# A two-layer graph attention kernel: the order of work in its first two and last two batches

## The chip, the core and the metric

The kernel runs on one NeuronCore of a Trainium2 chip. The core has five engines with queues of their own: TensorE (PE in the profile; its weight loads are PEld), VectorE (DVE), ScalarE (ACT), GpSimd (POOL) and SyncE (SP), which here only issues DMAs. Each engine works through its own list of instructions in order and waits at semaphores for the others. The metric is the device time of one execution in microseconds (us), the median of several runs.

## What is computed

32 graphs of 512 nodes, 512 features, one adjacency matrix for all. All data are float32.

```python
# layer 0: graph attention, 512 -> 256 features, joined with h
h = X @ W
e = leaky_relu(h @ a[0] + (h @ a[1]).T, 0.2) + NEG * (1 - adj)
x = layernorm(X + concat([softmax(e) @ h, h]))
# layer 1: 8 heads of 64, masked
q, k, v = (x @ Wq.T + bq), (x @ Wk.T + bk), (x @ Wv.T + bv)     # split into heads
scores = where(adj == 0, -inf, q @ k.T / 8)
x = layernorm(x + (softmax(scores) @ v) @ Wo.T + bo)
```

## The kernel before

One graph is a batch `b`. Its 512 nodes lie as 4 tiles of 128 rows, its features as 4 chunks of 128. The body at the end of the function is a program written out by hand: an opening (L892 to L925), a loop over 32 batches and the four head pairs `hp` of each (L941 to L1050), and an end (L1051 to L1056). All five engines keep the order in which these calls issue instructions (`manual_schedule`, L101), so the text order is the queue order on each engine.

**Layer 0.** `l0_project` multiplies a tile of x-transposed (`xt`) with `w_sb` into PSUM (`ph`, L276 by `matmul_f`) and ScalarE copies it to `h`. `w_sb` carries two more columns, `W @ a`, computed first (`pa`, L183). `l0_maxima`, `l0_scores` and `l0_weights` make the masked exponents `et`; `l0_values` multiplies them with `h` (`po`, L480) and adds to x; `l0_add_h` adds h to the other half of x on GpSimd; `ln_stats`, `ln_root` and `l0_norm` are the layer norm. For batch 0 rows are turned by TensorE (`row_of`: `pn`, `pself`, `pl`), for later ones through DRAM.

**Layer 1.** x is turned: for batch 0 by TensorE (`x1_first`: `px` L512, copied by ScalarE at L513), for later ones by VectorE in 32x32 blocks (`x1_blocks`) and 16 DMAs (`move_one`, L348). The products with the weights use a Strassen-like scheme with seven instead of eight block products: `x1_sums` makes four sums of x blocks (`tx`), `weight_sums` the sums of the weights (`wqx_sb`, `wkx_sb`, `wvx_sb`; `output_sums` for `wox_sb`), one quarter of each weight is negated by ScalarE. `project_two` gives q and k of two pairs (`pw`, L548), `project_v` v (`pv`, L624), `finish_seven` the output product (`pf`, L772) as a generator of ten steps that the loop calls one by one.

**A head pair.** `head_scores` computes 128 rows for two heads (`ps`, L701), VectorE subtracts the maximum under the mask (`minus_max`, L324) and ScalarE takes the exponent with its sum (L710). `head_blocks` turns the eight 128x512 blocks: VectorE in 32x32 blocks (L339), then 16 DMAs of 128 KB (`move_pair`, L356) put the blocks in place in `pt`. They go by SP; for pair 2 of batch 0 and the last two pairs of the last batch also by GpSimd and ScalarE. The sums are inverted, written to DRAM (L721) and read back to all partitions (`head_inverse`, L731, issued by GpSimd). One pair later `head_values` multiplies `pt` with v (`pav`, L740), and VectorE scales the result (L752).

**The end.** The output of the last batch isn't done by seven products: `finish` multiplies three chunks under the last pair's DMAs and the fourth after it (L841), then VectorE adds x, takes the statistics and normalises, tile by tile.

**Buffers.** `ps_m` and `ps_s` are four PSUM banks each, handed round by the tags "m" and "s". `t` and `pt` have one buffer each, so a pair's VectorE blocks wait until the pair before has been moved, and a move waits for the `pav` before.

```python
            if hp == 2 and b == 0 or hp >= 2 and not more:
                queues.append(nc.gpsimd)
            if not more and hp == 3:
                queues.append(nc.scalar)
            head_blocks(b, hp, queues)
            if before is not None:
                head_values(*before)
```

Of the kernel before, what the change touches and what calls it, by code (L numbers as in the profile page):

```python
# [14 lines left out]
P = 128  # L15
G = 32
# [10 lines left out]
def kernel(  # L27
# [123 lines left out]
    nc.sync.dma_start(w_sb[:, :, 2:], w.rearrange("(c p) o -> p c o", p=P))  # L151
# [3 lines left out]
    a_sb = const.tile([P, OC, 2], F32, name="a_sb")  # L155
    nc.sync.dma_start(a_sb, a)
    load_xt(0)
    adj_sb = prob.tile([P, NB, N], adj.dtype, name="adj_sb", tag="t", bufs=1)
    nc.sync.dma_start(adj_sb, adj.rearrange("(c p) n -> p c n", p=P))
    load_x(0)  # L160
    for dst, src in ((wq_sb, wqt), (wk_sb, wkt), (wv_sb, wvt)):
        nc.sync.dma_start(dst, src.rearrange("(c p) d -> p c d", p=P))
    load_xt(1)

    adjp_sb = act.tile([P, NB, N], adj.dtype, name="adjp_sb", tag="x1t")
# [59 lines left out]
    def weight_sums():  # L225

        for c in range(FC):
            nc.scalar.activation(wq_sb[:, c, :], wq_sb[:, c, :], AF.Identity, scale=SCALE)  # L230
        pairs = "p c (s i d) -> p i c s d"
        for w_t, x_t, view, s in (
            (wq_sb, wqx_sb, pairs, 2),
            (wk_sb, wkx_sb, pairs, 2),
            (wv_sb, wvx_sb, "p c (s i d) -> p i c (s d)", 1),
        ):
            v = w_t.rearrange(view, s=s, i=2)
            lo, hi = slice(0, FC // 2), slice(FC // 2, FC)

            i, j = (1, 0) if s == 2 else (0, 1)  # L240
            a11, a21 = v[:, i, lo], v[:, j, lo]
            a12, a22 = v[:, i, hi], v[:, j, hi]
            s1, s2, s4 = (x_t[:, i] for i in range(3))
            nc.vector.tensor_tensor(s1, a21, a22, ALU.add)
            nc.scalar.activation(a22, a22, AF.Identity, scale=-1.0)
            nc.vector.tensor_tensor(s2, s1, a11, ALU.subtract)
            yield
            nc.vector.tensor_tensor(s4, a12, s2, ALU.subtract)
            nc.vector.tensor_tensor(a21, a11, a21, ALU.subtract)
            yield  # L250

    def output_quarters():
        v = wo_sb.rearrange("p c (i d) -> p i c d", i=2)
        lo, hi = slice(0, FC // 2), slice(FC // 2, FC)
        return v[:, 0, lo], v[:, 0, hi], v[:, 1, lo], v[:, 1, hi]

    def output_sums():

        a11, a12, a21, a22 = output_quarters()
        s1, s2, s4 = (wox_sb[:, i] for i in range(3))  # L260
        nc.gpsimd.tensor_tensor(s1, a21, a22, ALU.add)
        nc.gpsimd.tensor_tensor(s2, s1, a11, ALU.subtract)
        nc.gpsimd.tensor_tensor(s4, a12, s2, ALU.subtract)
        nc.gpsimd.tensor_tensor(a21, a11, a21, ALU.subtract)
        nc.scalar.activation(a22, a22, AF.Identity, scale=-1.0)

    def output_weights():

        a11, _, a21, a22 = output_quarters()
        nc.gpsimd.tensor_tensor(a21, a11, a21, ALU.subtract)  # L270
        nc.scalar.activation(a22, a22, AF.Identity, scale=-1.0)
# [6 lines left out]
    def psum(name):  # L278
        return ps_m.tile([P, N], F32, name=name, tag="m")

# [71 lines left out]
    def move_pair(dst, t, queues):  # L352

        for g in range(4):
            for r in range(4):
                queues[(4 * g + r) % len(queues)].dma_start(  # L356
                    dst[r * G : (r + 1) * G, g], t[g * G : (g + 1) * G, r]
                )
# [8 lines left out]
    def l0_project(b, i):  # L367

        if i == 0:
            h_sb = act.tile([P, NB, F1 + 3], F32, name=f"h_{b}", tag="h")  # L370
            nc.gpsimd.memset(h_sb[:, :, F1 + 2 :], 1.0)
            st["h", b] = h_sb
        xt_sb, h_sb = st["xt", b], st["h", b]
        ph = ps_m.tile([P, 2 + F1], F32, name=f"ph_{b}_{i}", tag="m")
        matmul_f(ph, lambda c: xt_sb[:, c, i * P : (i + 1) * P], lambda c: w_sb[:, c, :])
        nc.scalar.copy(h_sb[:, i, : F1 + 2], ph)
# [20 lines left out]
    def l0_maxima(b):  # L397
# [4 lines left out]
        if b == 0:  # L402
            pn, mask = psum("pn"), st["mask0"]
# [41 lines left out]
    def l0_scores(b, tiles=range(NB)):  # L445

        h_sb = st["h", b]
        if b == 0:
            pself = psum("pself")
# [14 lines left out]
    def l0_row_first():  # L464
        most, row = st["least", 0], psum("pl")
# [9 lines left out]
    def l0_values(b, i):  # L475
        h_sb, z = st["h", b], st["x1", b]
        et = st["et", b]
        po = ps_m.tile([P, F1 + 1], F32, name=f"po_{b}_{i}", tag="m")
# [25 lines left out]
    def x1_first():  # L504
# [3 lines left out]
        for i in range(NB):  # L508
            px = psum(f"px_{i}")
# [177 lines left out]
    def head_scores(b, hp, i):  # L687
        qk = st["qk", b, hp]
        if i == 0:
            st["t", b, hp] = prob.tile(  # L690
                [P, 4, 2, FC, NB, G], F32, name=f"t_{b}_{hp}", tag="t", bufs=1
            )
# [3 lines left out]
        t, total = st["t", b, hp], st["tot", b, hp]  # L696
        pss = []
        for j in range(2):
            rows = slice(j * D, (j + 1) * D)
            ps = ps_s.tile([P, N], F32, name=f"ps_{b}_{hp}_{i}_{j}", tag="s")  # L700
# [14 lines left out]
    def head_blocks(b, hp, queues=(nc.sync,)):  # L715
        t, total = st.pop(("t", b, hp)), st.pop(("tot", b, hp))
        for j, i, p in st.pop(("p", b, hp)):
            transpose_blocks(t[:, :, j], i, p)
# [3 lines left out]
        st["inv", b, hp] = d  # L722
        pt = prob.tile([P, 4, 2, FC, NB, G], F32, name=f"pt_{b}_{hp}", tag="pt", bufs=1)
        move_pair(pt, t, queues)
# [111 lines left out]
    def finish(b, i, chunks=range(FC)):  # L836
        if 0 in chunks:
            st["pf", b, i] = psum(f"pf_{b}_{i}")
        ps, z = st["pf", b, i], st["x1", b]
        for c in chunks:  # L840
            nc.tensor.matmul(  # L841
                ps,
                st["ot", b, c // 2][:, c % 2, i * P : (i + 1) * P],
                wo_sb[:, c, :],
                start=(c == 0),
                stop=(c == FC - 1),
            )
        if FC - 1 not in chunks:
            return
        nc.vector.tensor_tensor(z[:, i, :], ps, z[:, i, :], ALU.add)  # L850
        o = out[b].rearrange("(c p) f -> p c f", p=P)
        layernorm(z, f"1_{b}_{i}", [i])
# [44 lines left out]
    l0_add_h(0)  # L897
    l0_row_first()
    l0_weights(0)
    nc.vector.tensor_scalar(bqs_sb, bq_sb, SCALE, None, ALU.mult)  # L900
    sums = weight_sums()
    next(sums)
    next(sums)
    for i in range(NB):
        l0_values(0, i)
        ln_stats(st["x1", 0], "0_0", i)
        ln_root("0_0", [i])
        if i > 0:
            l0_norm(0, [i - 1])
    l0_norm(0, [NB - 1])  # L910
    next(sums)
    next(sums)
    masks1()
    l0_project(1, 0)
    l0_project(1, 1)
    x1_first()
    l0_project(1, 2)
    l0_project(1, 3)
    l0_columns(1)
    x1_sums(0, nc.vector)  # L920
    steps(sums)
    steps(project_two(0, 0))
    l0_maxima(1)
    l0_write(1)
    l0_read(1)  # L925
    def l0_output(b):
# [13 lines left out]
    before = None  # L940
    for b in range(B):  # L941
        more = b < B - 1
        seven = finish_seven(b - 1) if b > 0 else None
        for hp in range(NP):
# [5 lines left out]
            if hp == 0:  # L950
                values = project_v(b)
                next(values)
                if more:
                    l0_scores(b + 1, [0, 1])
            elif hp == 1:
# [11 lines left out]
            else:  # L967
                if b > 0:
                    if not more:
                        steps(seven)  # L970
                        output_weights()
                    out_stats(b - 1)
                else:
                    output_sums()
# [13 lines left out]

            queues = [nc.sync]
            if hp == 2 and b == 0 or hp >= 2 and not more:  # L990
                queues.append(nc.gpsimd)
            if not more and hp == 3:
# [123 lines left out]
```

## Time and profile before

| what | value |
|---|---|
| three runs, us | 3106.84, 3104.37, 3106.60; median 3106.6 |
| profiled execution, us | 3105.46, of which its span is 3103.7 |
| mean granted TensorE clock | 0.991 |
| busy share: PE, PEld, DVE, ACT, POOL | 98%, 66%, 81%, 49%, 40% |
| chain that ended last | PE 91%, DVE 2%, DMA 2% |
| busy in 0 to 30 us: PE, DVE, ACT, POOL | 16.86, 12.76, 8.35, 9.17 |
| busy in 30 to 55 us | 19.86, 14.85, 9.18, 0.10 |
| busy in 3042 to 3082 us | 29.84, 23.38, 16.39, 14.65 |
| busy in 3082 to 3103.7 us | 8.94, 9.88, 1.18, 0.00 |

In the profile a group of instructions is written as line, engine, operation, output tile <- input tiles, shape and count; times run from the start of the span. In brackets stands how long the engine had been idle before, and who released it. A float32 matmul appears as two records, a transpose by TensorE as one.

### The profile page before, as it was taken

The numbers are of one execution on the slowest core, as the hardware profiler recorded it, in microseconds if no ns is written. First come the engines' busy times: TensorE is split into PE (matmuls) and PEld (weight loads), VectorE is DVE, ScalarE is ACT, GpSimd is POOL, SyncE is SP. The second block draws the span as 40 slices with busy tenths as digits, with TensorE's granted clock in tenths as the row PEclk, the third lists the DMA queues.
The fourth block names the chain that finished last, engine by engine and source line by source line (L and its number), as shares of the span: only waits on it lengthen the run. The fifth ranks groups of instructions, "written<-read, shape, count | busy, mean of one in ns | idle before, by whom it ended". The sixth has DMA issues, their size and how long they took to land.

```text
span 3103.7 us, 44628 instructions
## 1 busy us (share of the span) xinstructions
PE 3033.9 (98%) x13356; PEld 2058.0 (66%) x13356; DVE 2516.3 (81%) x5735; ACT 1527.4 (49%) x3246; POOL 1250.3 (40%) x1237
## 2 busy tenths in 40 slices
PE   7899999999999999999999999999999999999996
PEld 6566676666666666666666666666666666666653
DVE  5788788887788888788888888888888888888865
ACT  3445544455544455555455445455444555444542
POOL 1444444434444433434443434343444344444322
PEclk9999999999999999999999999999999999999998
DMA  5556665666665666755665756666656666656544
GB/s 163 123 141 161 154 163 140 160 154 156 163 155 136 167 154 151 172 143 142 162 162 142 176 140 154 153 163 150 165 138 160 153 158 162 153 139 166 141 120 113
DMA packets 247936, 470.92 MB, mean 152 GB/s; under 512 B 95568, under 2 KB 98128, under 8 KB 247696
## 3 DMA queue, kind: packets, MB, share of 16 engines
q1 hardware_dynamic: 233984, 430.82, 56.7%
q0 software_dynamic: 13472, 36.59, 4.5%
q8 instruction: 108, 1.77, 0.3%
q14 instruction: 132, 1.08, 0.1%
q10 hardware_dynamic: 240, 0.66, 0.1%
HBM read 132.65 MB, written 34.27 MB: 54 GB/s over the span
## 4 chain that ended last, share of the span: by engine, by line
PE 91%; DVE 2%; DMA 2%; SPq 1%; POOL 1%; issue 1%; ACT 0%; DVEq 0%; POOLq 0%; ACTq 0%
PE pw L548 24%; PE pav L740 14%; PE ps L701 14%; PE pf L772 12%; PE pv L624 12%; PE po L480 7%; PE ph L276 7%; SPq L356 1%; DMA pt<-t 1%; DVE t L339 1%; DMA d_least<-least 1%; DVE p L324 1%; DVE qk L585 0%; POOL x L795 0%; DVE stats L289 0%
## 5 line engine op out<-in xcount | busy, mean ns | idle before, releaser
L710 ACT ACTIVATE p<-p,least 128x512 f32<-128x512 f32 x1024 | 725.8, 711 | 517.1 <-DVE least L324 210.0
L324 DVE CUSTOM_DVE_ANT_0 p<-ps,mask 128x512 f32<-128x512 f32 x1024 | 644.7, 685 | 212.4 <-PE ps L701 212.3
L339 DVE STREAM_TRANSPOSE t<-p 128x512 f32<-128x512 f32 x1024 | 622.8, 674 | 14.2 <-issue 7.2
L701 PE MATMUL ps<-qk 64*128 64x512 f32 x2048 | 514.6, 617 | 3.8 <-DVE qk L585 3.4
L740 PE MATMUL pav<-pt,v 128*64 128x512 f32 x2048 | 474.8, 606 | 29.0 <-DMA pt<-t 16.9
L740 PEld LDWEIGHTS pav<-pt,v 128*64 128x64 f32 x2048 | 140.9, 138 | 348.6 <-issue 306.2
L731 POOL DMA_DIRECT2D inv<-d_tot x256 | 133.1, 525 | 559.1 <-DMA d_tot<-tot 297.9
L701 PEld LDWEIGHTS ps<-qk 64*128 64x128 f32 x2048 | 180.4, 186 | 211.9 <-issue 150.5
L462 POOL TENSOR_TENSOR et<-et,mask0t 128x512 f32<-128x512 f32 x126 | 143.8, 1153 | 327.1 <-ACT et L458 327.1
L480 PE MATMUL po<-h,et 128*128 128x257 f32 x1024 | 237.3, 390 | 6.7 <-ACT et L473 4.4
L276 PE MATMUL ph<-w_sb,xt 128*128 128x258 f32 x1024 | 235.8, 388 | 2.3 <-ACT x1t L513 2.0
L480 PEld LDWEIGHTS po<-h,et 128*128 128x128 f32 x1024 | 193.1, 194 | 63.4 <-issue 25.9
L795 POOL TENSOR_TENSOR x<-x,u_o 128x512 f32<-128x512 f32 x93 | 117.0, 1272 | 285.3 <-ACT u_o L790 254.9
L276 PEld LDWEIGHTS ph<-w_sb,xt 128*128 128x128 f32 x1024 | 194.1, 192 | 54.0 <-PE ps L701 22.0
L295 ACT ACTIVATE rstd<-mv,eps 128x4 f32<-128x4 f32 (+1 forms) x70 | 20.7, 297 | 357.3 <-DVE mv L290 352.8
L537 POOL TENSOR_TENSOR x<-x,bo_sb 128x512 f32<-128x512 f32 x128 | 158.4, 1269 | 91.2 <-DVE x1t_b L339 91.1
L710 ACT ACTIVATION_READ_ACCUMULATOR p<-p,least 128x1 f32 x1024 | 192.3, 188 | 0.0
L710 ACT ACT_TABLE_LOAD x63 | 80.8, 1283 | 221.5 <-DVE least L324 221.0
L772 PE MATMUL pf<-wo_sb,ot 128*128 128x256 f32 x744 | 182.9, 389 | 0.0
L289 DVE BATCH_NORM_STATS2 stats<-x 128x6 f32<-128x512 f32 x256 | 174.6, 682 | 6.1 <-POOL x L795 1.2
L772 PEld LDWEIGHTS pf<-wo_sb,ot 128*128 128x128 f32 x744 | 136.7, 190 | 63.9 <-issue 24.2
L772 PE MATMUL pf<-wox_sb,ot 128*128 128x256 f32 x744 | 179.1, 383 | 0.0
(145 smaller groups left out, 5346.8 us busy)
## 6 DMA issues: line engine op xcount, KB each, us to landing
pt<-t SPq DMA_DIRECT2D x2022, 128.0 KB, 3.5
x<-in_x_dram SPq DMA_DIRECT2D x32, 1024.0 KB, 5.7
inv<-d_tot POOLq DMA_DIRECT2D x256, 128.0 KB, 3.9
xt<-in_xt_dram SPq DMA_DIRECT2D x31, 1024.0 KB, 5.6
x1t<-x1t_b SPq DMA_DIRECT2D x496, 64.0 KB, 2.0
out_dram<-x SPq DMA_DIRECT2D x31, 1024.0 KB, 5.8
rows<-d_att SPq DMA_DIRECT2D x31, 512.0 KB, 4.0
rows<-d_least SPq DMA_DIRECT2D x31, 256.0 KB, 4.7
```

The source lines that it names most:

```text
L276: nc.tensor.matmul(ps, lhs(c), rhs(c), start=(c == 0), stop=(c == FC - 1))
L289: nc.vector.bn_stats(stats, z[:, i, :])
L324: nc.vector.tensor_tensor_reduce(out=out, in0=scores, in1=mask, scale=-1.0, scalar=MIN_INIT, op0=ALU.add, op1=ALU.min, accum_out=least,)
L339: nc.vector.transpose(t[:, :, :, i, :].rearrange("p r c q -> p c r q"), src.rearrange("p (c r k) -> p c r k", r=4, k=G),)
L480: nc.tensor.matmul(po, et[:, j, i * P : (i + 1) * P], h_sb[:, j, 2:], start=(j == 0), stop=(j == NB - 1),)
L537: nc.gpsimd.tensor_tensor(z[:, i, :], z[:, i, :], bo_sb, ALU.add)
L548: nc.tensor.matmul(ps[:, k * half : (k + 1) * half], weights(k, c), moving(c), start=start and k == 0 and c == 0, stop=c == FC // 2 - 1, s ...
L624: nc.tensor.matmul(ps[:, k * half : (k + 1) * half], columns(k, c), weights(c), start=start and k == 0 and c == 0, stop=c == FC // 2 - 1, ...
L701: nc.tensor.matmul(ps, qk[rows, 0, i * P : (i + 1) * P], qk[rows, 1, :], start=True, stop=True)
L710: nc.scalar.activation(p, p, AF.Exp, bias=least, scale=-1.0, accum_out=total[:, j, i : i + 1])
L740: nc.tensor.matmul(po[j * D : (j + 1) * D, :], st["v", b, c // 2][:, c % 2, head * D : (head + 1) * D], pt[:, :, j, c, :, :].rearrange("p ...
L772: nc.tensor.matmul(ps[:, k * half : (k + 1) * half], columns[:, c, k * P : (k + 1) * P], weights(c), start=start and k == 0 and c == 0, st ...
```

## The change

1. Loads: `a`, `wt`, `w` instead of `w`, `wt`, `a`; xt of batch 1 straight behind `adj`, before x of batch 0; the key weights before the query weights. The second form of the mask (`adjp_sb`) shares a buffer with `adj_sb` under the tag "t", no longer with x1t.
2. `l0_project` is split into product and copy. Two of batch 1's four products stand after `l0_add_h(0)`, one after `l0_row_first`, one after the last `l0_values` of batch 0; the ScalarE copies follow together. Batch 0's other PSUM tiles of layer 0 move to `ps_s`.
3. Sums of the key and query weights run on GpSimd, those of the value weights on VectorE after `x1_sums`; ScalarE's negations are calls of their own. `masks1` and `l0_maxima(1)` stand later; `l0_add_h(1)` earlier.
4. The output weight's negation moves from before batch 0's last projection to the end of pair 3. Pair 2 of batch 0 is moved by SP alone.
5. Pairs (30, 2), (31, 2) and (31, 3) are turned by TensorE (`head_turn`), into `ps_s` banks, and copied out by VectorE and ScalarE in turns. No blocks and no DMAs for them.
6. For batches 30 and 31 the last steps of `finish_seven` run in pair 3; in batch 31 its GpSimd step stands after `project_two` instead of before it.
7. The last output: x is added in PSUM by a product with the identity, statistics are read from PSUM, and ScalarE normalises from PSUM, one tile behind.

```diff
-    nc.sync.dma_start(w_sb[:, :, 2:], w.rearrange("(c p) o -> p c o", p=P))
+    a_sb = const.tile([P, OC, 2], F32, name="a_sb")
+    nc.sync.dma_start(a_sb, a)
...
+    nc.sync.dma_start(w_sb[:, :, 2:], w.rearrange("(c p) o -> p c o", p=P))
     load_xt(0)
...
     nc.sync.dma_start(adj_sb, adj.rearrange("(c p) n -> p c n", p=P))
+    load_xt(1)
     load_x(0)
-    for dst, src in ((wq_sb, wqt), (wk_sb, wkt), (wv_sb, wvt)):
+    for dst, src in ((wk_sb, wkt), (wq_sb, wqt), (wv_sb, wvt)):
...
-    load_xt(1)
...
+    def weight_sums(which, engine):
+
+        a11, a12, a21, a22 = weight_quarters(which)
+        s1, s2, s4 = (which[1][:, i] for i in range(3))
+        engine.tensor_tensor(s1, a21, a22, ALU.add)
+        engine.tensor_tensor(s2, s1, a11, ALU.subtract)
+        engine.tensor_tensor(s4, a12, s2, ALU.subtract)
+        engine.tensor_tensor(a21, a11, a21, ALU.subtract)
+
+    def weight_negative(which):
+
+        a22 = weight_quarters(which)[3]
+        nc.scalar.activation(a22, a22, AF.Identity, scale=-1.0)
...
+    def head_turn(b, hp):
+
+        pt = prob.tile([P, 4, 2, FC, NB, G], F32, name=f"pt_{b}_{hp}", tag="pt", bufs=1)
+        for k, (j, i, p) in enumerate(st.pop(("p", b, hp))):
+            ps = psum_s(f"pt_{b}_{hp}_{i}_{j}")
+            for c in range(FC):
+                cols = slice(c * P, (c + 1) * P)
+                nc.tensor.transpose(ps[:, cols], p[:, cols], ident)
+            (nc.vector.tensor_copy if k % 2 == 0 else nc.scalar.copy)(
+                pt[:, :, j, :, i, :].rearrange("p g c q -> p c g q"),
+                ps.rearrange("p (c g q) -> p c g q", c=FC, g=4),
+            )
+        head_sums(b, hp)
+        st["pt", b, hp] = pt
...
+    def last_products(b, i):
+
+        ps = st["pf", i] = psum(f"pf_{b}_{i}")
+        nc.tensor.matmul(ps, ident, st["x1", b][:, i, :], start=True, stop=False)
+        for c in range(FC - 1):
+            last_product(b, i, c)
...
+    def last_norm(b, i):
...
+        nc.vector.bn_stats(stats, ps)
+        nc.vector.bn_aggr(mv, stats)
+        nc.scalar.activation(rstd, mv[:, 1:2], AF.Sqrt, bias=eps)
+        yield
+        nc.vector.reciprocal(rstd, rstd)
+        nc.vector.scalar_tensor_tensor(shift, mv[:, 0:1], -1.0, rstd, ALU.mult, ALU.mult)
+        nc.scalar.activation(z[:, i, :], ps, AF.Identity, bias=shift, scale=rstd)
         nc.sync.dma_start(o[:, i, :], z[:, i, :])
...
     l0_add_h(0)
+    second = [l0_product(1, 0), l0_product(1, 1)]
     l0_row_first()
+    second.append(l0_product(1, 2))
     l0_weights(0)
...
-    sums = weight_sums()
-    next(sums)
-    next(sums)
+    for c in range(FC):
+        nc.scalar.activation(wq_sb[:, c, :], wq_sb[:, c, :], AF.Identity, scale=SCALE)
+    weight_sums(KEYS, nc.gpsimd)
+    weight_negative(KEYS)
+    weight_sums(QUERIES, nc.gpsimd)
     for i in range(NB):
         l0_values(0, i)
         ln_stats(st["x1", 0], "0_0", i)
+        if i == NB - 1:
+            second.append(l0_product(1, 3))
+            for k in range(NB):
+                l0_copy(1, k, second[k])
...
-    masks1()
-    l0_project(1, 0)
-    l0_project(1, 1)
     x1_first()
-    l0_project(1, 2)
-    l0_project(1, 3)
     l0_columns(1)
     x1_sums(0, nc.vector)
-    steps(sums)
-    steps(project_two(0, 0))
+    weight_sums(VALUES, nc.vector)
+    masks1()
+    two = project_two(0, 0)
+    next(two)
+    weight_negative(VALUES)
+    next(two)
+    next(two)
     l0_maxima(1)
     l0_write(1)
     l0_read(1)
+    steps(two)
...
+    turned = {(B - 2, 2), (B - 1, 2), (B - 1, 3)}
...
+                if b == 0:
+                    l0_add_h(1)
...
+                    if b + 2 >= B:
+                        steps(seven)
                     if not more:
-                        steps(seven)
                         output_weights()
...
-                    output_sums()
+                    weight_sums(OUTPUT, nc.gpsimd)
...
-            queues = [nc.sync]
-            if hp == 2 and b == 0 or hp >= 2 and not more:
-                queues.append(nc.gpsimd)
-            if not more and hp == 3:
-                queues.append(nc.scalar)
-            head_blocks(b, hp, queues)
+            if (b, hp) not in turned:
+                head_blocks(b, hp)
             if before is not None:
                 head_values(*before)
+            if (b, hp) in turned:
+                head_turn(b, hp)
...
-                if b > 0:
+                if b > 0 and more:
                     next(seven)
...
+                if not more:
+                    next(seven)
...
                 if b == 0:
+                    weight_negative(OUTPUT)
                     add_bias(1)
...
     for i in range(NB):
-        finish(b, i, range(FC - 1))
-    head_values(b, 3, lambda name: ps_s.tile([P, N], F32, name=name, tag="s"))
+        last_products(b, i)
+    head_values(b, 3, psum_s)
+    norms = []
     for i in range(NB):
-        finish(b, i, [FC - 1])
+        last_product(b, i, FC - 1)
+        norms.append(last_norm(b, i))
+        next(norms[i])
+        if i > 0:
+            steps(norms[i - 1])
+    steps(norms[NB - 1])
```

## The prediction

> **What bounds the kernel.** I read the two strips of the page first, TensorE's busy share and its granted clock, in 40 slices.
>
> ```profile
> span 3103.7 us, 44628 instructions
> PE   7899999999999999999999999999999999999996
> PEclk9999999999999999999999999999999999999998
> ```
>
> TensorE is full from the second slice to the last but one. The table of stretches shows 100.00 busy in each 100 us that I asked for between 190 and 2945 (one: 99.46). The change leaves the order of that middle alone, so I expect nothing there, and only the first 155 us and the last 160 us count. The timeline of TensorE gives its waits there (start, length, instruction, idle before and releaser):
>
> ```profile
> 49.21 6.30 PE L276 MATMUL ph<-w_sb,xt 128*128 128x258 f32 x16 [2.04 <-ACT x1t L513]
> 55.35 1.02 PE L548 MATMUL pw<-x1t,wq_sb 128*128 128x256 f32 x4
> ...
> 93.41 8.98 PE L480 MATMUL po<-h,et 128*128 128x257 f32 x28 [3.27 <-ACT et L473]
> ...
> 149.72 5.46 PE L740 MATMUL pav<-pt,v 128*64 128x512 f32 x16 [6.19 <-ACT h L376]
> ```
>
> ```profile
> 2968.93 5.56 PE L740 MATMUL pav<-pt,v 128*64 128x512 f32 x16 [6.79 <-DMA pt<-t]
> 3033.40 2.99 PE L701 MATMUL ps<-qk 64*128 64x512 f32 x8 [3.37 <-DVE qk L585]
> 3061.41 5.40 PE L740 MATMUL pav<-pt,v 128*64 128x512 f32 x16 [5.82 <-DMA pt<-t]
> 3081.89 5.35 PE L740 MATMUL pav<-pt,v 128*64 128x512 f32 x16 [3.16 <-DMA pt<-t]
> ```
>
> The first block is the opening: half of batch 1's projection runs late (6.30 us for 16 records, where 32 take 7.24 later), the first `pw` follows it, then come two long waits. The second is the end: three waits for blocks that DMA turns, one for a sum on GpSimd. Each wait costs more than itself: 16 records of L740 take 3.65 us elsewhere and 5.4 here. The stretches of 0.5 us (length, TensorE busy, clock, DMA) say why:
>
> ```profile
> 23.50:24.00 0.50, 0.00 (x0) 1.00 1.04 385
> 27.00:27.50 0.50, 0.00 (x0) 0.60 1.07 262
> 33.50:34.00 0.50, 0.50 (x3) 0.57 1.12 221
> ```
>
> The clock falls to 0.50 at 27.1, after idle 22.0 to 25.9 and 26.5 to 28.7, and is back at 33.9, so 5.2 us of matmuls run at half pace. The falls near 47.6, 92.0, 2966, 3058 and 3082 look alike and hold it down for 3.4 to 5.2 busy us: a gap of 3 us or more costs another **1.7 to 2.6 us**.
>
> **Opening, up to the first `pw`.** Up to 22.0 the start hangs on adj landing at 16.6; the reordered loads keep adj behind the same 2 MB. Then:
> - Two tiles of the second projection stand before `pl` (25.89): 16 of 32 records that take 7.24 us warm, 3.6 us, fill 22.0 to 25.6. The third (1.8 us) fills 26.5 to 28.3. The clock should stay up, so `po` runs at 1.8 us a tile from 28.7, waits for its exponents until 30.5, and ends at 36.3 instead of 38.3; the fourth ends at 38.1. xt(1) takes the place of x(0), which was issued at 7.81 and landed 11.5 later, at 19.3; x(0) moves to the next slot (10.91 + 11.1 = 22.0), before GpSimd wants it (25.1). Cost nothing while these slots hold; 3 us if xt(1) came after 25.
> - VectorE loses the query sums (32.56 to 35.23) and the key sums (44.41 to 47.07), 2.7 us each. Its norm chain starts with `po` at 31.2: 4 tiles x 1.61 us (recip, 256-wide add, stats, aggregate) + 4 x 0.66 us norms + 0.4 us for the root's table = 40.7, instead of 44.4.
> - GpSimd takes 8 sums behind its four `x+h` adds (end 28.66). Nearest row: L261 to L264, 1.27 us each, so 10.1 us to 38.8. Queued behind them is only a memset. The first wanted is the query sum, at the third product, 1.75 us after `pw` starts (41.8 below): 4.7 us slack.
> - ScalarE copies the four projections after the last exponents, with no wait for VectorE; the transposes `px` follow at 38.1 in other banks. The last x1t copy (0.51 us) ends near 41.8.
>
> [...] The row:
>
> ```profile
> 112.43 1.92 DVE L305 TENSOR_SCALAR x<-x,mv,rstd 128x512 f32<-128x512 f32 x4
> 2933.42 3.78 DVE L305 TENSOR_SCALAR x<-x,mv,rstd 128x512 f32<-128x512 f32 x4
> ```
>
> Alone, four norms take 1.92; with GpSimd working, 3.78: 0.46 us more each. Two or three norms fall beside the sums. [...] by the row 1.2 at most; I take 0.7. So `pw` starts at 42.5: **12.9 us gained.**
>
> **Opening, from `pw` to the third pair.** The 12.2 us of `pw` are unchanged. Behind it VectorE has the value sums and masks1 (3.9 us) under those products. The wait at 71.6 shrinks with 1.6 us (`ps` to the value products 6.98 us before, 5.4 now), and gaps of 0.5 go: 15.0 gained at `ps` of pair 1 (85.63, now 70.6). `x+h` of batch 1 now stands before the row on GpSimd (3.6 us), so VectorE's v results wait for the row (2.15) and the p7 sum (1.4), then come two L472, two masks (2.25) and the exponents. `po` can start near 75.5 with TensorE idle from 72.5: 3.0 us, and the clock likely falls. Before it was 4.4 us with the same fall, so +1.7 with rounding: `po` ends at 85.6 instead of 102.3, **16.7 gained**.
>
> Pair (0,2) now goes by SP alone. SP's chain from pair 1's turned blocks has no slack: 16 pt x 0.64, xt 0.6, 16 x1t 12.2, then:
>
> ```profile
> 136.71 6.01 SPq L356 DMA_DIRECT2D pt<-t  x8
> 131.93 3.91 POOL L356 DMA_DIRECT2D pt<-t  x8 [16.09 <-DMA x1t<-x1t_b]
> ```
>
> Before, GpSimd issued half, and the output sums behind these issues held ScalarE's h copies, so `pav` started at 149.72. Now 16 x 0.64 from 136.7 end at 147, landing 3.8 later (row: 2964.79, 3.84), 150.7. Moving the negation frees ScalarE, but the transfer takes that wait's place: -1.0 (bounds -3.5 and +1.5, if x1t goes faster without GpSimd's half). **Opening: 15.7.** What follows runs cold in both.
>
> **End, batch 30.** Turning pair (30,2) costs 32 transposes. 16 of L206 took 2.09 us, four of L363 start 0.44 apart; 0.11 each, 3.5 us, with one bank wait 3.7. The copies (ScalarE L513 0.51, VectorE L210 0.69, four each) lie beside. `pav` no longer waits 6.79. But the products moved to hp 3 put GpSimd's last two adds behind the inv issues and the tx sums (L527 to L530, 5.1 us from 2960): they end at 2967.6. VectorE's stats, minus-max, ScalarE's exponents and out_norm (2.9) queue behind, so the copy p1 that `pw`'s fourth product waits for comes at 2977.7; TensorE, 5.9 us ahead, idles from 2973.8 and goes cold. The last turned pair by DMA, (30,3), leaves VectorE at 2977 instead of 2973.6 and lands at 2991.9, just when `pav` wants it. **Net 0** (-1 to +3).
>
> **End, batch 31.**
> - GpSimd's `to`/`ot` sums move behind p7: it is added by 3026.4 instead of 3031.7, q and k are ready by 3028.2, `ps` follows at 3030.0: 3.37 idle and 1.8 of slow clock gone, +5.2.
> - `pav` (31,1) then waits for its DMA (issues end 3032.9, +3.8): -0.7. Turning (31,2): -3.7. `pav` (31,2) starts at once, without 5.82 idle and 1.8 slow: +7.6. Here 8.3 us ahead, `pav` ending at 3058.4.
> - Turning (31,3): ScalarE's four copies stand behind its four out_norm instructions, which end at 3064.7; transposes 6 to 8 wait for these banks, end 3066.6. TensorE goes cold (2.5).
> - The products that used to lie under the DMA wait (12 of 0.86 us) now stand alone, and 4 identity products of that shape are added: 16 x 0.86 = 13.8. Then `pav` 3.6, ot 1.1: 3087.6 against 3088.3 before. Ahead 0.7.
> - The tail. Before, ot's end to the last norm was four VectorE rounds of 2.7 us. Now VectorE has stats, aggregate, two small ones (1.2 us a tile) and ScalarE normalises from PSUM (L870 0.73, L513 0.51): 7.2 us instead of 12.0; the store's 3.4 stay. +4.8.
>
> **End: 5.5.** [...]
>
> **Sum.** 15.7 + 5.5 = 21.2. The profiled execution took 3105.46 (span 3103.7), which gives 3084.3; the median, 3106.6, is 1.1 above it: **3085.4**.
>
> **Rivals.**
> 1. Forecast, 0.60, own range 3080 to 3091.
> 2. The opening shift is eaten by SP's single queue and by `po`'s exponents: landings at 0.76 us each (the x1t pace) cost 2 more, GpSimd's row 2 to 3 more. For it: SP has no slack there. Against: less runs beside it. Gain 10.5 + 5.5: 3090.5. 0.18.
> 3. The turned pairs give their waits back: [...] 15.7 - 2: 3092.9. 0.11.
> 4. Neither gap lets the clock fall, and x1t is faster: 3079. 0.08.
> 5. Slower: [...] `pw`'s third product waits for them; beyond 4.7 us slack each us costs one. To eat 21 us they must take 4.5 us each; at 5.5 the time is 3113. Every such sum in the trace takes 1.26 to 1.5. 0.03.
>
> A difference under 0.2% (6.2 us) can't be told from no change. Faster 0.94, same 0.03, slower 0.03. The range, 3077 to 3095, leaves some 2 in 10 out.
>
> **What would show it.** First `pw` near 42 to 43 with clock 1.00 from 20 to 72; a wait at `po` of 3 us; `pav` (0,2) released by DMA pt; no idle before `pav` (30,2), but one inside `pw` of batch 31 released by ScalarE's copy; `ps` (31,2) without idle; the last store within 11 us of the last ot. I am wrong if `pw` starts after 46, or if the middle changes its pace.

## The result, and the profile after

The changed kernel takes **3078.89 us** (median of 6 runs, 3075.24 to 3080.89) against 3106.22 before (6 runs), ratio 0.9913, 95% interval [0.9901, 0.9926]: 27.3 us less, where 21.2 were forecast. That lies inside the stated range of 3077 to 3095, but 1.1 us under the forecast's own 3080 to 3091; rival 4 had named 3079. The profiled execution took 3080.21 us, with a span 25.3 us shorter than before. The strips of its page:

```profile
span 3078.4 us, 44731 instructions
...
PE   8999999999999999999999999999999999999998
...
PEclk9999999999999999999999999999999999999999
```

The last slice went from 6 to 8 and the last clock digit from 8 to 9. TensorE's timeline in the opening (start, length, instruction, idle before and releaser):

```profile
35.94 1.91 PE L264 MATMUL ph<-w_sb,xt 128*128 128x258 f32 x8
...
40.28 1.28 PE L509 MATMUL px<-ident,x 128*128 128x128 f32 x8 [1.56 <-DVE rstd L291]
42.23 2.07 PE L545 MATMUL pw<-x1t,wq_sb 128*128 128x256 f32 x4 [0.67 <-ACT x1t L510]
...
78.21 9.21 PE L477 MATMUL po<-h,et 128*128 128x257 f32 x32 [2.86 <-ACT et L470]
...
133.55 5.77 PE L757 MATMUL pav<-pt,v 128*64 128x512 f32 x16 [4.99 <-DMA d_att<-att]
```

The projection's tiles have left the place in front of `pw`, which starts 13.1 us earlier. But four records of L545 take 2.07 us there and 1.03 later: the clock is down, which it was not before. The end:

```profile
2962.88 2.05 PE L545 MATMUL pw<-tx,wqx_sb 128*128 128x256 f32 x4 [4.75 <-ACT p L569]
...
3024.83 3.90 PE L736 MATMUL pt<-ident,p 128*128 128x128 f32 x32
3028.57 1.89 PE L789 MATMUL pf<-wox_sb,ot 128*128 128x256 f32 x8
...
3046.39 1.23 PE L736 MATMUL pt<-ident,p 128*128 128x128 f32 x8 [1.23 <-DVE pt L737]
...
3063.69 3.65 PE L757 MATMUL pav<-pt,v 128*64 128x512 f32 x16
3068.49 3.70 PE L861 MATMUL pf<-wo_sb,ot 128*128 128x512 f32 x8 [1.15 <-DVE ot L769]
```

Of the four waits shown before none is left. New are 4.75 us inside batch 31's first projection, and 2.4 us in three pieces inside the turn of the last pair (the largest is shown). A turned pair costs 3.90 us, and the rows behind it run at full clock.

Where the time went, in us gained, read from the starts of the same instruction in both traces (the first four rows count from the start, the others are stretches):

| stretch | forecast | measured |
|---|---|---|
| to the first `pw` | 12.9 | 13.1 |
| to the first scores of pair (0,1) | 15.0 | 12.3 |
| to the end of `po` of batch 1 | 16.7 | 15.0 |
| to the values of pair (0,2) | 15.7 | 16.2 |
| from there to the values of (30,1) | 0 | -0.3 |
| from there to batch 31's first scores | 0 | -1.4 |
| from there to the last eight products | +0.7 | +5.4 |
| from these to the end of the span | +4.8 | +5.4 |
| sum of the last five rows | 21.2 | 25.3 |

### The profile page after: what moved, and what is told of

The parts are those of the page before. It is cut to its first block, busy times and chain, and to the rows that moved or that the text cites. A ratio compares the mean times of both kernels' runs of the same rounds, so it can differ in the third digit from the quotient of the medians.

```text
span 3078.4 us, 44731 instructions
## 1 busy us (share of the span) xinstructions
PE 3039.4 (99%) x13460; PEld 2065.7 (67%) x13460; DVE 2490.8 (81%) x5711; ACT 1537.7 (50%) x3262; POOL 1251.6 (41%) x1224
## 5 line engine op out<-in xcount | busy, mean ns | idle before, releaser
L330 DVE STREAM_TRANSPOSE t<-p 128x512 f32<-128x512 f32 x1000 | 607.7, 674 | 10.2 <-issue 5.5
```

The lines of the kernel that those rows point to most:

```text
L330: nc.vector.transpose(t[:, :, :, i, :].rearrange("p r c q -> p c r q"), src.rearrange("p (c r k) -> p c r k", r=4, k=G),)
```

## The experiments

Two limits on reading them. Runs of one kernel mostly differ by some 3 us either way, in run 12 by up to 7. And the stretch from the values of pair (0,3) to those of (30,1), the same order in all, took from 2771.7 to 2777.9 us in twelve profiled runs of kernels with the changed opening or a variant of it; why it varies isn't known. So a part of a few us is read from its own stretch of the trace, and the medians say whether the whole agrees.

**1. The opening alone.** The end is set back to the old one.

```diff
-    turned = {(B - 2, 2), (B - 1, 2), (B - 1, 3)}
+    turned = set()
...
-        last_products(b, i)
+        finish(b, i, range(FC - 1))
...
```

> The changed kernel's opening (loads, projection in the gaps, weight sums on GpSimd, masks, first move of pair 2 on one queue) with the old end: no pair is turned by TensorE, the last norm is the old one. The two ends of the kernel are 2900 us apart and share only the engines' queues. Theory 'two separate gains': the opening is worth what the two traces differ by at the first product of pair (0,2), 149.7 - 133.5 = 16.2 us, so 3106.2 - 16 = 3090 us (3088 to 3092). Rival 'one gain through the clock or the DMA queues': a part of what looks like the opening's gain only lasts to the end because the end was changed too, so under 12 us here (over 3094). A second rival, that the opening's lead is eaten in the 29 batches between: under 3 us (over 3103).

Measured 3087.52 us, ratio 0.9941 [0.9928, 0.9953], 17.9 below the runs beside it and 0.5 under the range. The gain lasts to the end by itself. TensorE's timeline in this run shows something else, though the opening is the same code:

```profile
39.41 1.28 PE L509 MATMUL px<-ident,x 128*128 128x128 f32 x8 [1.55 <-DVE rstd L291]
41.37 1.13 PE L545 MATMUL pw<-x1t,wq_sb 128*128 128x256 f32 x4 [0.68 <-ACT x1t L510]
...
75.63 7.56 PE L477 MATMUL po<-h,et 128*128 128x257 f32 x32 [2.85 <-ACT et L470]
```

The gaps are those of the changed kernel to 0.01 us, yet `pw` takes 1.13 in place of 2.07 and `po` 7.56 in place of 9.21. Here the scores of pair (0,1) come at 70.80, where 70.6 was forecast. That they agree is partly luck: `pw` is 1.1 us earlier than forecast in this run, and from it to these scores it takes 29.4 us, where 28.1 were forecast (31.1 in the changed kernel).

**2. The end alone.** The old opening, with the turned pairs and the new last norm.

```diff
+    turned = {(B - 2, 2), (B - 1, 2), (B - 1, 3)}
...
-            if hp == 2 and b == 0 or hp >= 2 and not more:
+            if hp == 2 and b == 0:
...
```

> The old opening with the changed end: pairs (30,2), (31,2) and (31,3) turned by TensorE, the last norm from PSUM. Theory 'two separate gains': what the traces differ by behind pair (30,1), -1.3 in batch 30, +5.4 from there to the last product, +5.4 in the tail, is 9.5 us, so 3106.2 - 9.5 = 3096.7 us (3095 to 3099); together with the kernel that has the opening alone the gains add up to the whole 27.3 us within 1.5 us. Rival: the end's gain hangs on the opening's rearranged buffers or queues, then the two gains add up to less than 24 us.

3095.19 us, ratio 0.9967 [0.9956, 0.9979]: 10.2 less. 17.9 + 10.2 = 28.1 against 27.3 for the whole. The two gains add up, as expected.

**3. Batch 29's norm late.**

```diff
-                    out_stats(b - 1)
+                    if b + 2 != B:
+                        out_stats(b - 1)
...
+                if b + 2 == B:
+                    out_stats(b - 1)
                 if more:
                     steps(project_two(b + 1, 0))
                 head_inverse(b, 3)
+                if b + 2 == B:
+                    ln_root(f"1_{b - 1}")
+                    out_norm(b - 1)
+                    store(b - 1)
```

> In batch 30 alone, the statistics of batch 29's last norm are put behind the values of pair (30,2) on VectorE, and its root, its four norms on ScalarE and its store behind the projection of batch 31. Theory 'queue of ScalarE': the 4.75 us idle before the fourth product of that projection (released by ScalarE's copy, which stands behind late exponentials and four norms of 2.9 us) and the cold rows behind it (2.05 + 1.91 + 1.56 us in place of 3 x 1.03) go, 4.75 + 2.4 = 7.2 us; about 1 may come back where VectorE's statistics (3.3 us) now stand ahead of the projection's results: 3071.5 to 3074, around 3072.5. Rival 'the cold clock is set elsewhere' (by the turned pair before it): the wait goes and the rows stay cold, 3074 to 3075. Rival 'the projection waits for GpSimd's sums tx anyway': under 2 us gained, over 3077.

3069.92 us, ratio 0.9888 [0.9872, 0.9903]. The timeline of the stretch (TensorE and ScalarE):

```profile
2953.59 1.03 PE L545 MATMUL pw<-tx,wk_sb 128*128 128x256 f32 x4
2954.45 1.03 PE L545 MATMUL pw<-tx,wqx_sb 128*128 128x256 f32 x4
...
2956.98 1.28 ACT L286 ACT_TABLE_LOAD   x1
...
2961.45 1.99 PE L699 MATMUL ps<-qk 64*128 64x512 f32 x8
```

No idle time ahead of the fourth product (the second row), no cold row; the root's table load comes behind the copies. From the values of (30,2) to the scores of batch 31 it takes 15.9 us (2945.59 to 2961.45) in place of 23.1 (2949.09 to 2972.23): **7.3 gained, 7.2 expected**. The profiled run gained another 3.7 us in the opening: it is the second in which the clock stayed up there (scores of pair (0,1), third and fourth tile, at 83.62; changed kernel 87.35). That would explain why the time lies under the expected range.

**4. The same stall from GpSimd's side.** The norms stay; the sums `tx` go behind the last two adds.

```diff
                     if b + 2 >= B:
                         steps(seven)
+                    if b + 2 == B:
+                        x1_sums(b + 1, nc.gpsimd)
...
-                if more:
+                if b + 2 < B:
                     x1_sums(b + 1, nc.gpsimd)
```

> The changed kernel with one order swapped on GpSimd in batch 30: the four sums tx for batch 31's projection stand behind the last two adds of batch 29's output, in place of ahead of them. The norms of batch 29 stay where they are on ScalarE. If GpSimd's order sets the stall of batch 30's end, VectorE's statistics no longer wait 3.0 us for the second add, so the exponentials, the norms and the copies come about 3 us earlier: the idle time before the projection's fourth product falls from 4.75 to about 1.7 us, and the clock behind it may stay whole: 2.5 to 5.5 us gained from the first product of that projection to the first scores of batch 31 (19.55 us in the changed kernel). If the norms in front of the copies are enough by themselves, the stretch stays at 18 us or more. If the projection now waits for tx, its third product shows a wait for GpSimd and nothing is gained.

3075.58 us, ratio 0.9898 [0.9882, 0.9915]. TensorE's timeline:

```profile
2961.01 1.10 PE L545 MATMUL pw<-tx,wqx_sb 128*128 128x256 f32 x4 [1.59 <-ACT p L569]
```

The wait falls from 4.75 to 1.59 us, and the clock stays; from the values of (30,2) to the scores of batch 31 it takes 17.7 us in place of 23.1, 5.4 less. So GpSimd's queue made some 3.2 us of the wait, and what is left of it goes with ScalarE's order (run 3). Both halves of the forecast's chain are shown.

**5. No turn in batch 30.**

```diff
-    turned = {(B - 2, 2), (B - 1, 2), (B - 1, 3)}
+    turned = {(B - 1, 2), (B - 1, 3)}
...
-                    if b + 2 >= B:
-                        steps(seven)
                     if not more:
+                        steps(seven)
                         output_weights()
...
```

> The changed kernel with pair (30,2) moved by DMA and batch 29's output finished in pair 2, as in the kernel before; batch 31's pairs stay turned. Theory 'the turn of batch 30 does not pay in the changed kernel': what the traces show from pair (30,1)'s values to the first scores of batch 31 is 40.2 us before and 41.5 after, so this kernel is 1.3 us faster than the changed one: 3077 to 3079 us, against 3078.9, and 6 us slower than the one with batch 29's norms late. Rival 'the turn pays': without it the wait for the DMA of pair (30,2) comes back (6.8 us idle and cold rows behind it) and something else is late as well, 3081 us or more.

3078.97 us, ratio 0.9907 [0.9892, 0.9921]. The wait for the DMA is back, in TensorE's timeline:

```profile
2953.95 5.06 PE L757 MATMUL pav<-pt,v 128*64 128x512 f32 x16 [6.46 <-DMA pt<-t]
```

From the values of (30,1) to the scores of batch 31 it takes 39.3 us; the changed kernel takes 41.5, the one with the late norm 34.2. In the changed kernel this turn loses 2.2 us; turn and late norm together gain 5.1. A late norm without the turn was not run.

**6. Batch 30's norm late.**

```diff
-            if b > 0 and hp == 3:
+            if b > 0 and hp == 3 and more:
                 out_norm(b - 1)
...
                 head_turn(b, hp)
+            if hp == 3 and not more:
+                out_norm(b - 1)
```

> In batch 31 alone, batch 30's four norms on ScalarE (2.9 us) are put behind the four copies of turned pair (31,3). Theory: the turn takes 6.7 us since its fifth to eighth tiles wait for PSUM banks that ScalarE's copies free too late; with the copies right behind the last exponential (3046.8) the last tile is turned at about 3048.4 in place of 3049.9, so 1.4 us gained: 3077 to 3078 us. Rival: the exponentials themselves, or VectorE's copies, are last, then nothing is gained (3078.9). Rival: the norms, now behind, delay the last products through the table load for the root, then slower (over 3080).

3076.40 us, ratio 0.9905 [0.9891, 0.9918]. From the values of (31,2) to the last eight products it takes 27.5 us (3039.33 to 3066.85) in place of 28.9: 1.4 gained, as expected.

**7. The old last norm.** The last eight products are followed by the old add, statistics and norm on VectorE; the identity products go.

```diff
-        last_products(b, i)
+        finish(b, i, range(FC - 1))
...
```

> The changed kernel with the old last norm: the residual added by VectorE from PSUM to SBUF, statistics from SBUF, the norm on VectorE; no product with the identity. Theory 'the tail': from the first of the last eight products to the end of the span 15.3 us come back in place of 9.9, less the 4 x 0.86 us that the identity products took of TensorE in front of the last values, so the span is 5.4 - 3.4 = 2.0 us longer: 3080 to 3082 us. Rival 'the identity products are free, hidden under the wait for the last pair's sums or tiles': then 5.4 us longer, 3084.

3079.27 us, ratio 0.9909 [0.9895, 0.9924]. In the trace the last eight products stand 25.5 us behind the values of (31,2) (28.9 with the new norm: 3.4 for four identity products, as expected), and 15.0 us follow them (9.9). The new norm nets 1.7 us, which the medians can't tell.

**8. The move of pair (0,2) on two queues again.**

```diff
...
-                head_blocks(b, hp)
+                head_blocks(b, hp, (nc.sync, nc.gpsimd) if (b, hp) == (0, 2) else (nc.sync,))
```

> The changed kernel with the one part of its opening undone that I had counted as a loss: the sixteen moves of pair (0,2) go by SP and GpSimd in turn, as before, in place of SP alone. In the changed kernel's trace SP issues them from 120.82 to 130.87, and the pair's values start at 133.55 after 4.99 us of idle time, cold (5.77 us). GpSimd stands idle there from 101 to 123.6, so half the issues end at about 125.8 and land by 129.5. Theory 'the issue rate of one queue sets this wait': idle time 1 us or none, clock whole, 4 + 2 = 6 us gained, 3072 to 3075 us. Rival 'the transfers themselves, 2 MB on 16 engines, set it': they land at the same time, the same 3078.9. Rival 'GpSimd's sums for the next projection, now 4 us later, are waited for in its stead': under 2 us.

All three fell: 3086.59 us, ratio 0.9933 [0.9920, 0.9945], **slower** than the changed kernel: no run of the one reaches a run of the other, though the two intervals just touch. The values of (0,2) do come earlier, 131.76 in place of 133.55, but 22 us later the timeline shows:

```profile
145.33 6.00 DVE L315 CUSTOM_DVE_ANT_0 junk<-pn,mask 128x512 f32<-128x512 f32 x1
145.84 4.93 POOL L534 TENSOR_TENSOR x<-x,bo_sb 128x512 f32<-128x512 f32 x4
151.26 0.68 DVE L315 CUSTOM_DVE_ANT_0 junk<-pn,mask 128x512 f32<-128x512 f32 x1
...
154.19 2.08 PE L699 MATMUL ps<-qk 64*128 64x512 f32 x4 [5.14 <-DVE qk L582]
```

One maximum on VectorE takes 6.00 us, its neighbour 0.68: it lasts until GpSimd, first at two issues and then at four adds of the bias, is through (150.77). The eight issues made GpSimd some 2.7 us late, and with it the copy `pn` (142.51, before 139.81) that these maxima read, so that they met the adds. The projection's results stand behind them, the scores wait 5.14 us and start cold. By the values of (0,3) the run is 4.7 us behind the changed kernel; of the 7.7 us between the medians this part shows 4.7, and the rest isn't explained.

**9. The projection late.**

```diff
-    second = [l0_product(1, 0), l0_product(1, 1)]
...
+    l0_project(1, 0)
+    l0_project(1, 1)
     x1_first()
+    l0_project(1, 2)
+    l0_project(1, 3)
     l0_columns(1)
```

> The changed kernel with the second batch's projection back at its old place, behind the norms and around the transposes of the first batch; the weight sums stay on GpSimd. Theory: the four groups (7.2 us warm) come back into the path, of which 3.6 us now lie behind the last norm, and the two gaps open again, so the clock falls under the first values: the first product of the first projection comes 7 to 9 us later than 42.2, at 49 to 51, and the time is 3086 to 3088 us. Rival 'the weight sums carry the opening's gain, the projection was hidden anyway': under 4 us lost.

3085.74 us, ratio 0.9926 [0.9914, 0.9939]. The expectation of `pw` at 49 to 51 was wrong; TensorE's timeline:

```profile
28.41 8.85 PE L477 MATMUL po<-h,et 128*128 128x257 f32 x32 [1.88 <-POOL x L379]
37.09 3.65 PE L264 MATMUL ph<-w_sb,xt 128*128 128x258 f32 x16
40.58 2.05 PE L509 MATMUL px<-ident,x 128*128 128x128 f32 x16
42.46 3.65 PE L264 MATMUL ph<-w_sb,xt 128*128 128x258 f32 x16
45.95 1.02 PE L545 MATMUL pw<-x1t,wq_sb 128*128 128x256 f32 x4
```

The first half of the projection lies beside VectorE's norms, which TensorE waits for anyway; only the second half is in the path, and `pw` comes 3.7 us late. With TensorE busy up to it, `pw` is warm, so only 1.9 of that is left at pair (0,1) and 0.6 at the values of (0,3). So of the 6.9 us between the medians the opening explains 0.6; the middle of the profiled run was the longest of the twelve, for no cause that these runs show.

**10. The sums on VectorE.**

```diff
-    weight_sums(KEYS, nc.gpsimd)
+    weight_sums(KEYS, nc.vector)
...
-    weight_sums(QUERIES, nc.gpsimd)
...
     l0_norm(0, [NB - 1])
+    weight_sums(QUERIES, nc.vector)
+    weight_negative(QUERIES)
```

> The changed kernel with the sums of the query and key weights back on VectorE, the keys' ahead of the first values and the queries' behind the last norm; the projection stays in the gaps. Theory: VectorE's chain is what the transposes and the first projection wait for, so 2.7 us of key sums push the norms and 2.7 us of query sums push the sums tx: 3 to 6 us lost, the first product of the first projection at 44 to 46, or a wait at its third product for tx: 3082 to 3085 us. Together with the kernel with the late projection it should lose the 12.5 to 13 us that the first projection moved ahead. [...]

3085.85 us, ratio 0.9931 [0.9918, 0.9945]. `pw` waits longer:

```profile
43.95 2.08 PE L545 MATMUL pw<-x1t,wq_sb 128*128 128x256 f32 x4 [2.53 <-ACT x1t L510]
```

It starts 1.7 late, and pair (0,1) 2.9 late. This part is about as expected, though the median lies 0.9 beyond the range; the sum of the two is not: 1.9 + 2.9 = 4.8 us at pair (0,1) of the 12.3 gained. This fits two chains, TensorE's products and VectorE's, that run beside each other: undoing one lengthens the path only by what it sticks out beyond the other. A kernel with both undone was not run, nor one with the order of the loads alone undone, so what the loads gave is open.

**11. Both norms late, the turn behind the first row of last products.** On top of the edit of run 3:

```diff
     for i in range(NB):
         last_products(b, i)
+        if i == 0:
+            head_turn(b, 3)
+            head_inverse(b, 3)
+            out_norm(b - 1)
+            store(b - 1)
...
```

> Two fixes on top of the changed kernel. Batch 29's statistics, root, norms and store behind the projection of batch 31 as in the run that had this alone (7.2 us in its trace); and in batch 31 the turn of pair (31,3) behind the first row of the last products, with batch 30's norms behind it. Theory: the turn's waits (1.23 + 0.28 + 0.88 us idle) are filled by 3.4 us of products, 2.4 to 3 us gained, so 3078.9 - 7.2 - 2.7 = 3069 us (3067 to 3071). Rival: the turn moved back delays the sums of pair (31,3), or banks of PSUM that the last products hold, and the values of (31,3) wait: then no better than 3071.7.

3071.49 us, ratio 0.9887 [0.9872, 0.9901]. The turn now takes 3.66 us in one piece:

```profile
3041.06 3.66 PE L736 MATMUL pt<-ident,p 128*128 128x128 f32 x32
```

From the values of (31,2) to the last eight products it takes 25.8 us in place of 28.9: 3.1 gained. The time is 0.5 us beyond the expected range and close to the rival's 3071.7, but the rival's wait isn't there: the values of (31,3) start without idle time.

**12. The same, with batch 1's weights ahead of three values results.** On top of run 11:

```diff
         result(0, 0, b2, p1)
+        yield
         result(0, 1, b3, u2)
...
+                if b == 0:
+                    next(values)
+                    l0_weights(1)
                 steps(values)
...
```

> The kernel with both late norms and the turn behind the first row of last products, and one order more changed in the opening: batch 1's weights on VectorE stand behind the first of the four values results of batch 0 in place of behind all four. Theory: the exponents that the first values of batch 1 wait for come about 2 us earlier, the wait of 2.85 us before them falls below 1, and the clock, which fell behind it in eight of the ten profiled runs with this opening, stays up: from the first scores of pair (0,1) to the third, 13.9 us with the clock fallen and 12.3 without, becomes 10.5 to 11: span 3065 to 3068, median 3066 to 3070 us. Rival: the values of batch 1 need PSUM banks that the postponed results still hold, so the wait only changes its name and the stretch stays above 12 us.

3073.64 us, ratio 0.9890 [0.9876, 0.9904]: no gain. `po` still waits 2.84 us, and not for the cause that I or the rival had named. The timeline of this run:

```profile
73.64 2.27 POOL L459 TENSOR_TENSOR et<-et,mask0t 128x512 f32<-128x512 f32 x2
73.70 4.57 DVE L469 TENSOR_TENSOR et<-et,row 128x512 f32<-128x512 f32 x4
76.56 2.38 ACT L470 ACTIVATE et<-et 128x512 f32<-128x512 f32 x4 [4.54 <-DVE et L469]
```

In the changed kernel the four subtractions on VectorE are:

```profile
76.35 2.80 DVE L469 TENSOR_TENSOR et<-et,row 128x512 f32<-128x512 f32 x4
```

Counted from the scores of pair (0,1), VectorE reaches them 1.8 us earlier, and they take 4.57 us in place of 2.80. The first alone takes 2.77 and ends behind GpSimd's masks, which end at 75.9; the first exponent follows the scores of pair (0,1) by 4.05 us, as it does in the changed kernel (4.07). So GpSimd's order seems to be the bound here; moving its masks was not tried.

Runs 3, 11 and 12 have the lowest medians, and their intervals overlap almost wholly, so no order among them is settled. The 3.1 us of run 11 are shown in the trace only.

## Why the prediction was right, and where not

- **The sum.** The total lies in the range, but several terms were off, in both directions: in the traces the opening brought 0.5 us more than forecast and the end 4.0. The other 2.0 of the 27.3 us between the medians are not between the profiled spans. Rival 4's 3079 was met by luck, since its two reasons failed: the clock fell in the opening, and the sixteen x1t moves take 12.1 us, 12.2 before.
- **Opening, to the first `pw`:** 12.9 and 13.1. The products went into the gaps, `po` ran at 1.9 us a tile, the sums held one norm up (1.07 us in place of 0.55; 0.7 us of delay allowed).
- **"Clock 1.00 from 20 to 72"** failed. From `pw` to the scores of pair (0,1) 2.1 us more were to be gained, and 0.9 were lost. Of these 3.0 the clock made 1.7. The rest is a wait that shrank less than forecast (from these first scores to the value products 6.98 us became 6.04, not 5.4), and gaps of 0.5 us that stayed. The stretches of 0.5 us of the changed kernel (window and its length, TensorE's busy time and instructions, its clock, DMA's share and GB/s):

```profile
38.50:39.00 0.50, 0.22 (x3) 1.00 0.78 295
39.00:39.50 0.50, 0.00 (x0) 1.00 0.37 139
39.50:40.00 0.50, 0.00 (x0) 1.00 0.17 61
...
42.00:42.50 0.50, 0.27 (x1) 0.77 0.00 0
42.50:43.00 0.50, 0.50 (x2) 0.50 0.00 0
...
45.50:46.00 0.50, 0.50 (x4) 0.82 0.00 0
```

  I had counted only gaps of 3 us or more. Filling the old gaps left TensorE waiting in front of the transposes and `pw`, 1.56 + 0.67 us, and from 38.7 to 42.2 it is busy for 1.3 us. In eight of the ten profiled runs with this order up to `pw` the clock fell there, and again at the 2.85 us before `po`; in two it fell at neither. The rows put the fall at 42.27 and the return at 45.68, 3.41 us later; the next fall, at 79.82, lasts as long (to 83.23). The first row below is the 3.41 us that end with the fall at 42.27. The other two are stretches of that length around the same gaps in run 1, where the clock stayed:

```profile
38.86:42.27 3.41, 1.29 (x9) 1.00 0.11 43
...
36.90:40.31 3.41, 1.83 (x15) 1.00 0.70 257
40.31:43.72 3.41, 2.73 (x15) 1.00 0.09 17
```

  In these rows one stretch holds both gaps in the changed kernel, and each of the two in run 1 holds one of them. In the changed kernel's trace the clock falls four times with products still to come, and TensorE is busy for 0.88 to 1.61 of the 3.41 us ahead; in that of the kernel before eight times, with 0.00 to 1.24. So the same gaps cost nothing in run 1 and some 3.4 us here (1.7 at `pw`, 1.7 at `po`). What decides between the two is not shown: the gaps alone could not tell me.
- **`po`:** 3.0 us idle forecast, 2.86 measured; end 85.6, measured 87.4; it starts 2.7 us late, 1.7 of them for the clock at `pw`. The shorter wait was put at 1.7 us, while its own terms, 4.4 and 3.0, give 1.4.
- **Pair (0,2):** 15.7 and 16.2, near by luck: `po` ended 1.7 us behind the forecast, and the single queue, taken as a loss of 1.0, gained 1.2. The last move took 3.0 us to land, where 3.8 were taken. The row names the DMA `d_att`, the next in SP's queue behind the sixteen moves (issued 120.82 to 130.87) that were forecast as the releaser; both land at about 133.4. Run 8 shows that the other way is worse, for a reason that I hadn't seen.
- **Batch 30:** "net 0 (-1 to +3)" became -1.4. The chain named (adds, statistics, exponents, norms, copy, fourth product) is shown by runs 3 and 4; the wait, forecast at 3.9 us, took 4.75.
- **Batch 31:** 8.3 (8.4 by its own terms) and 9.0 up to the end of the values of (31,2); the wait for DMA at (31,1) that I took as -0.7 isn't there.
- **The end of batch 31** is the largest miss, 0.7 against 5.4. The step "transposes 6 to 8 wait for these banks" and "TensorE goes cold (2.5)" failed: ScalarE's copies start at 3049.52, when the last transposes already run, so the banks came from VectorE's copies, which give every second one back. The wait comes in three short pieces, the turn takes 6.7 us and not 8.2, and the clock never falls. 1.5 + 2.5 us, with the 0.7 above, are the difference.
- **The tail:** 4.8 and 5.4. The four identity products in front of it take 3.4 back (run 7).
- **Transposes and the clock.** Each turned pair is followed by rows at full speed, such as 1.89 at 3028.57. The last one is the strongest case: from 3043.19 to 3049.86 TensorE has nothing but transposes and waits, is busy for 4.29 of these 6.67 us, and the granted clock is 1.00. It is 1.00, too, from 40.5 on in run 1, behind the stretch from 36.90 to 40.31, which but for 0.1 us holds transposes and waits alone. In the kernel before TensorE has only transposes and waits from 19.2 on, and the clock stays at 1.00 until 27.1, where it falls with 0.62 us of work in the 3.41 ahead.

## What to carry to other kernels

An instruction moved off one engine joins a queue on another: ask which small copy stands behind it there, and whether TensorE waits for that copy; work that nobody waits for (here a finished batch's norm) goes behind it, and that alone brought 7.3 us more in the trace. Parts that shorten two chains side by side don't add up, so test them together and alone. Fill TensorE's gaps where the next product waits: two short gaps close together, 1.56 and 0.67 us between 38.7 and 42.2, still let the clock fall here in eight of ten profiled runs, and not in the other two.

## What the hardware showed that I had not expected

GpSimd held VectorE up for a whole series of instructions. I had reckoned with norms only, which lost some 0.5 us each (1.07 us in place of 0.55). Instructions with two inputs in SBUF lost far more: 6.00 us for a maximum that takes 0.68 (run 8), 4.57 for four subtractions that take 2.80 (run 12). Each of the two held up ended 0.56 us after GpSimd's row of four or two instructions had. Values results, which read one input from PSUM, ran beside the same masks at 0.67 each in the changed kernel.

It isn't always so. The 128 such maxima of the changed kernel take 0.67 to 1.80 us, so they lose about one GpSimd instruction (1.27 us) at most; and in its opening a VectorE product with both inputs in SBUF took 1.12 us, from 25.96 on, in the midst of four GpSimd adds (24.78 to 28.36). What let it in there, and not in run 8, no run shows.
